# First product of an MLP on one core: both blocks of a PSUM bank filled before ScalarE empties them

## The chip, the cores and the metric

The kernel runs on one core of one Trainium2 chip. The metric is device time in microseconds: from the start of the program to its end. Beside the runs that are only timed there is one execution taken by the hardware profiler; all durations of single instructions come from it. The engines are TensorE (PE, with its weight loads shown as PEld), VectorE (DVE), ScalarE (ACT), GpSimd (POOL) and the queue SyncE (SP) that issues the transfers.

## The reference

Four layers act on an image batch of 8 x 384 x 32 x 32, each with a normalisation ahead of it and a residual. Layers 0 and 2 are Mamba blocks with a selective scan over 1024 tokens, layer 1 is a gated filter with a depthwise convolution, and layer 3 is a depthwise convolution. The change is in the MLP at the end of layer 2:

```python
# layer 2, after the scan; t: (8, 1024, 384)
t = y @ out_proj_w.T
t = jax.nn.gelu(t @ mlp_w1.T + mlp_b1, approximate=False) @ mlp_w2.T + mlp_b2
# mlp_w1: (1536, 384), mlp_w2: (384, 1536)
x = x + t
```

All data is fp32.

## The kernel before

The batch is cut into chunks of T = 512 tokens, two per image, so 16 chunks pass through layers 0 and 1 and then 16 through layers 2 and 3. Each chunk has a main line of 24 steps (`QUADS`). A step multiplies and expands (`decay`: four small matmuls into the four `dA` banks and four exponentials on ScalarE), scans (`scan`: four scans on DVE, then products on DVE and POOL) and sums over the states (`gather`: four matmuls into `y`). Everything else is a *job*: a Python generator that yields pieces, such as `front` (projections, SiLU, step sizes), `gates`, `out_proj`, `mlp` and `layer3`.

The order on each engine's queue is the order in which the Python program issues (the schedule is manual), and semaphores are set for every dependency. Between the parts of a step, `Jobs.step` lets jobs issue pieces until a planned amount of work is used (`ROOM`). It counts matmul columns (`mm`) and DVE columns (`Meter`); ScalarE's work isn't counted.

PSUM has three banks for the jobs (`psg`, `NBANK = 3`), four for `dA` and one for `y`. `pipe` runs a list of units through stages: one stage per piece. With `deep=1` a piece runs the last stage of the unit in flight and then the first stage of the next one.

The MLP of a chunk works in two halves of TH = 256 tokens. In the first product, `up(f)` is a unit for two blocks of 128 outputs. Its two stages, `run(0)` and `run(1)`, fill columns 0 to 255 and 256 to 511 of one bank `ps_up`, with three matmuls each, and each then has ScalarE add the bias and write its block to `h1` (in the trace: `h<-ps_up`). So a piece issues, in this order: the matmuls of a unit's second block, its eviction, the matmuls of the next unit's first block, its eviction. Six units make a half. Then Gelu runs over `h1` in two instructions, with a load of its table before and of the exponential's table after (`exp_again`), and the second product (`ps_dn`) uses the result.

Weights come from HBM in parts of 384 KB (`mw`, four buffers); `take` hands one to a unit and asks for the part three further on. `mm` issues every matmul from line 177 and `act` every activation from line 241, so the profile is read by tile names. An fp32 matmul leaves two records in the trace.

Of the kernel before, what the change touches and what calls it, by code (L numbers as in the profile page):

```python
# [11 lines left out]
AF = mybir.ActivationFunctionType  # L12
# [41 lines left out]
def _flat(ap):  # L54
    return ap.rearrange("p a b -> p (a b)")
# [100 lines left out]
def tile_conv_preact_d4(ctx: ExitStack, tc: tile.TileContext, a: dict, out: bass.AP):  # L156
# [15 lines left out]
    def mm(out_, lhsT, rhs, start=True, stop=True):  # L172
        columns = 1
        for n in rhs.shape[1:]:
            columns *= n
        work[0] += columns / 600
        nc.tensor.matmul(out_, lhsT, rhs, start=start, stop=stop)  # L177
# [11 lines left out]
    def pipe(units, deep=2):  # L189


        flying = []
        units = deque(units)
        while units or flying:
            went = bool(flying)
            for f in list(flying):
                if f["stages"]:
                    f["stages"].popleft()(f["ps"])
                settle(f)
                if not f["stages"]:  # L200
                    flying.remove(f)
            if units and live["ps"] < NBANK and len(flying) < deep:
                went = True
                name, stages = units.popleft()
                live["ps"] += 1
                ps = psg.tile([P, 512], F32, tag="ps", name=name)
                stages[0](ps)
                f = {"stages": deque(stages[1:]), "ps": ps, "bank": True}
                settle(f)
                if f["stages"]:  # L210
                    flying.append(f)
            if units or flying:
                yield None if went else WAIT
# [8 lines left out]
    def both(*stages):  # L222


        def run(ps):
            for stage in stages:
                stage(ps)

        return run
# [3 lines left out]
    def act(out_, in_, func, **kw):  # L233

        if func in (AF.Exp, AF.Ln):
            if act_set["now"] != "exp":
                nc.scalar.preload_act_table_set(SET_EXP)
                act_set["now"] = "exp"
        elif func not in (AF.Identity, AF.Copy, AF.Square, AF.Abs):
            act_set["now"] = func  # L240
        nc.scalar.activation(out_, in_, func, **kw)  # L241

    def exp_again():

        nc.scalar.preload_act_table_set(SET_EXP)
        act_set["now"] = "exp"
# [610 lines left out]
    TH = T // 2  # L857
# [33 lines left out]
    def mlp(s):  # L891
        x = s["x"]
        loaded, more = s["weights"]
        first = True

        def take():

            nonlocal first
            if not first:
                more()  # L900
            first = False
            return loaded.popleft()

        for half in range(2):
            cols = slice(half * TH, (half + 1) * TH)
            h1 = p2.tile([P, NF, TH], F32, tag="h1", name="h1")

            def up(f):
                def run(q):
                    def run_q(ps):  # L910
                        if q == 0:
                            now[0] = take()
                        cols_q = slice(q * TH, (q + 1) * TH)
                        for k in range(KC):
                            mm(
                                ps[:, cols_q], now[0][:, q * KC + k, :],
                                s["t"][k][:, cols], start=k == 0, stop=k == KC - 1,
                            )
                        act(
                            h1[:, f + q, :], ps[:, cols_q], AF.Identity,  # L920
                            bias=b1[:, f + q : f + q + 1],
                        )

                    return run_q

                now = [None]
                return [run(0), run(1)]

            yield from pipe([("ps_up", up(f)) for f in range(0, NF, 2)], deep=1)
            yield EARLY  # L930
            for q in range(2):
                part = _flat(h1[:, q * NFH : (q + 1) * NFH, :])
                act(part, part, AF.Gelu)
            exp_again()
            yield NEXT

            def down(m):
                def sum_up(g, third):
                    def run(ps):
                        if third == 0:  # L940
                            now[0] = take()
                        for f in range(third * KC, (third + 1) * KC):
                            mm(
                                ps[:, :TH], now[0][:, f, :], h1[:, g * NFH + f, :],
                                start=g == 0 and f == 0, stop=g == 1 and f == NFH - 1,
                            )

                    return run

                now = [None]  # L950

                def add(ps):
                    xc = x[:, m, cols]
                    vector.scalar_tensor_tensor(
                        xc, ps[:, :TH], b2[:, m : m + 1], xc, ALU.add, ALU.add
                    )

                return [sum_up(0, 0), sum_up(0, 1), sum_up(1, 0), both(sum_up(1, 1), add)]

            yield from pipe([("ps_dn", down(m)) for m in range(KC)], deep=1)  # L960
# [46 lines left out]
    for t in range(total):  # L1007
# [19 lines left out]
        if t > 0:  # L1027
            p, q = steps[t - 1]
# [4 lines left out]
        if t + AHEAD < total:  # L1033
            p, q = steps[t + AHEAD]
# [138 lines left out]
```

## Time and profile before

| | |
|---|---|
| median of 3 runs | 7943.65 us (7939.29 to 7958.2) |
| the profiled execution | 7942.61 us, span 7940.8 us |
| mean granted TensorE clock, profiled execution | 0.919 |
| PE / DVE / ACT / POOL busy | 7334.3 / 5717.7 / 4052.0 / 5639.5 us |
| first and last `ps_up` matmul | 4094.5 us, 7849.5 us |
| `ps_up` matmuls, records and busy time | 2304, 605.4 us |
| `h<-ps_up` evictions | 384 of 474 ns mean, 177.3 us |

The span is the time between the first and last instruction that the profile shows; the 1.8 us that the execution is longer lie around it. Busy time is a union of the records of one engine. PE's ends are modelled, so a busy PE isn't PE at its peak. The last figures of a group's row in the profile are the engine's idle time just before the group's instructions and what ended most of it. The granted clock is the share of full speed at which TensorE ran.

### The profile page before, as it was taken

The page shows a single profiled execution, that of the slowest core. Times are in us where ns is not written, and L with a number is a line of the kernel's source. Part 1 is how long each engine was busy: PE and PEld are TensorE (multiplying, and loading weights), DVE is VectorE, ACT ScalarE, POOL GpSimd, SP SyncE. Part 2 cuts the span into 40 slices and gives each one's busy share as a digit, 9 for nine tenths or more (in the row PEclk, how much of TensorE's full clock was granted, in tenths as well). Part 3 has the DMA queues.
Part 4 walks back from the last instruction along what each step waited for, and adds up shares of the span by engine and source line. Part 5 has one row for each costly group of instructions (what it writes and reads, how often), then busy time and mean ns, then how long its engine had stood idle before and what let it go on. Part 6 is the DMA issues. An engine that isn't in the chain of part 4 may idle for free. (4 is left out here: it accounts for less than half of the span.)

```text
span 7940.8 us, 76871 instructions
## 1 busy us (share of the span) xinstructions
PE 7334.3 (92%) x25954; PEld 3037.2 (38%) x25954; DVE 5717.7 (72%) x7254; ACT 4052.0 (51%) x6980; POOL 5639.5 (71%) x2710
## 2 busy tenths in 40 slices
PE   7989999999998999989999989999899989999898
PEld 2223333333333333333334444444444444344445
DVE  5988788878787878778737647767767676676770
ACT  4445545555555555554544545555555555555553
POOL 5888888877787878777737746767767667676770
PEclk8888888989898999989889989999999999999999
DMA  5665655555564656556526645666656666565662
GB/s 138 148 148 137 144 135 136 134 133 137 133 149 118 146 129 143 122 141 151 122 69 173 159 121 144 154 158 165 157 134 163 166 149 159 138 171 140 168 157 65
DMA packets 289704, 1122.90 MB, mean 141 GB/s; under 512 B 37402, under 2 KB 91754, under 8 KB 191004
## 3 DMA queue, kind: packets, MB, share of 16 engines
q1 hardware_dynamic: 289308, 1117.98, 57.2%
q8 instruction: 205, 3.36, 0.2%
q14 instruction: 191, 1.56, 0.1%
HBM read 1042.34 MB, written 75.50 MB: 141 GB/s over the span
## 5 line engine op out<-in xcount | busy, mean ns | idle before, releaser
L623 POOL TENSOR_TENSOR g<-g,bc 128x1024 f32<-128x1024 f32 x1536 | 3586.5, 2357 | 181.3 <-DMA g<-dud 164.4
L660 POOL TENSOR_TENSOR g<-g,bc 128x1024 f32<-128x1024 f32 x768 | 1805.8, 2351 | 1609.5 <-DVE carry L656 871.8
L241 ACT ACTIVATE dA<-dA,w_A 128x512 f32<-128x512 f32 x3072 | 1858.3, 661 | 1480.3 <-PE dA L177 1467.3
L177 PE MATMUL dA<-dt,selr 32*128 32x512 f32 x6144 | 1521.9, 676 | 67.8 <-DVE g L654 59.2
L643 DVE TENSOR_TENSOR_SCAN dA<-dA,carry,g 128x512 f32<-128x512 f32 x768 | 986.7, 1285 | 750.5 <-issue 375.4
L643 DVE TENSOR_TENSOR_SCAN dA<-dA,g 128x512 f32<-128x512 f32 x768 | 940.8, 1225 | 554.3 <-ACT dA L241 221.6
L654 DVE TENSOR_TENSOR g<-dA,bc 128x512 f32<-128x512 f32 x1536 | 1054.5, 687 | 29.8 <-DVE dA L643 0.5
L177 PE MATMUL y<-g,sely 128*32 128x512 f32 x6144 | 934.2, 640 | 47.6 <-POOL g L660 42.4
L643 DVE TENSOR_TENSOR_SCAN g<-dA,carry,g 128x512 f32<-128x512 f32 x768 | 940.4, 1266 | 0.0
L643 DVE TENSOR_TENSOR_SCAN g<-dA,g 128x512 f32<-128x512 f32 x768 | 893.7, 1206 | 0.0
L177 PEld LDWEIGHTS dA<-dt,selr 32*128 32x128 f32 x6144 | 452.1, 192 | 947.2 <-DVE g L643 473.9
L177 PE MATMUL ps_up<-t,mw 128*128 128x256 f32 x2304 | 605.4, 411 | 144.4 <-ACT h L241 100.5
L177 PE MATMUL ps_dn<-h,mw 128*128 128x256 f32 x2304 | 566.1, 397 | 67.7 <-DMA mw<-in_l_mlp_w 55.9
L177 PE MATMUL ps_z<-xf,w_in 128*128 128x512 f32 x1152 | 590.0, 653 | 27.8 <-DVE dt L85 24.0
L177 PE MATMUL ps_dw<-tp,diag 96*96 96x512 f32 x1152 | 580.7, 645 | 14.3 <-ACT diag L241 14.3
L177 PEld LDWEIGHTS ps_up<-t,mw 128*128 128x128 f32 x2304 | 444.9, 201 | 371.0 <-ACT h L241 186.7
L177 PE MATMUL ps_in<-xf,w_in 128*128 128x512 f32 x1152 | 556.2, 623 | 25.3 <-DVE u L85 22.0
L177 PE MATMUL ps_out<-u,w_out 128*128 128x512 f32 x1152 | 548.7, 623 | 9.1 <-DVE x L85 9.1
L177 PEld LDWEIGHTS ps_dn<-h,mw 128*128 128x128 f32 x2304 | 436.7, 196 | 260.3 <-issue 121.0
L177 PE MATMUL ps_dw<-xp,diag 128*128 128x512 f32 x864 | 405.4, 620 | 41.0 <-ACT diag L241 40.9
L241 ACT ACTIVATE h<-ps_up,vec 128x256 f32<-128x256 f32 x384 | 177.3, 474 | 442.7 <-PE ps_up L177 442.4
L241 ACT ACTIVATE u<-ps_in,w_vec 128x512 f32<-128x512 f32 x192 | 149.4, 778 | 478.1 <-PE ps_in L177 478.1
(98 smaller groups left out, 6514.5 us busy)
## 6 DMA issues: line engine op xcount, KB each, us to landing
g<-dud SPq DMA_DIRECT2D x768, 1024.0 KB, 7.1
mw<-in_l_mlp_w SPq DMA_DIRECT2D x384, 384.0 KB, 7.2
dud<-du SPq DMA_DIRECT2D x768, 64.0 KB, 1.7
xk<-in_x SPq DMA_DIRECT2D x48, 256.0 KB, 4.1
xf<-in_x SPq DMA_DIRECT2D x16, 768.0 KB, 8.5
x<-in_x SPq DMA_DIRECT2D x16, 768.0 KB, 8.4
x_mid<-x SPq DMA_DIRECT2D x16, 768.0 KB, 4.7
xk<-x_mid SPq DMA_DIRECT2D x48, 256.0 KB, 5.4
```

Source lines behind the costliest of these rows:

```text
L177: nc.tensor.matmul(out_, lhsT, rhs, start=start, stop=stop)
L241: nc.scalar.activation(out_, in_, func, **kw)
L623: nc.gpsimd.tensor_mul(g, g, s["bc"][:, 0, :].unsqueeze(1).to_broadcast([P, 2, T]))
L643: nc.vector.tensor_tensor_scan(dAs[j] if j < own else g[:, j, :], dAs[j], g[:, j, :], 0.0 if s["c"] == 0 else carry[:, q : q + 1], ALU.mul ...
L654: nc.vector.tensor_mul(g[:, j, :], dAs[j], s["bc"][:, 1, :])
L660: nc.gpsimd.tensor_mul(g, g, s["bc"][:, 1, :].unsqueeze(1).to_broadcast([P, 4 - own, T]))
```

## The change

In `up`, the two evictions leave the stages that fill the blocks and are issued together, behind the second block's matmuls. A piece now issues: the matmuls of a unit's second block, both its evictions, the matmuls of the next unit's first block. What is computed, the tiles and the number of instructions stay the same.

```diff
@@ def up(f): @@
                                 ps[:, cols_q], now[0][:, q * KC + k, :],
                                 s["t"][k][:, cols], start=k == 0, stop=k == KC - 1,
                             )
+
+                    return run_q
+
+                def evict(ps):
+                    for q in range(2):
                         act(
-                            h1[:, f + q, :], ps[:, cols_q], AF.Identity,
+                            h1[:, f + q, :], ps[:, q * TH : (q + 1) * TH], AF.Identity,
                             bias=b1[:, f + q : f + q + 1],
                         )
 
-                    return run_q
-
                 now = [None]
-                return [run(0), run(1)]
+                return [run(0), both(run(1), evict)]
 
             yield from pipe([("ps_up", up(f)) for f in range(0, NF, 2)], deep=1)
```

`both` runs its stages one after the other on the same bank.

## The prediction

> **What bounds the kernel now.** First the page: busy shares, then the granted TensorE clock.
>
> ```profile
> PE 7334.3 (92%) x25954; PEld 3037.2 (38%) x25954; DVE 5717.7 (72%) x7254; ACT 4052.0 (51%) x6980; POOL 5639.5 (71%) x2710
> ...
> PEclk8888888989898999989889989999999999999999
> ```
>
> TensorE is busy for 92% of the span, no other engine for more than 72%. A busy PE isn't yet a limit, so I looked at the stretch in which the changed loop runs (from 4094 us; each row: length, then busy time of PE, PEld, DVE, ACT, POOL, then clock, DMA share, GB/s), and at what PE waits for there.
>
> ```profile
> 4094.00:7870.00 3776.00, 3449.04 (x13393) 1672.21 (x13392) 2508.79 (x3201) 1916.52 (x3150) 2475.44 (x1183) 0.95 0.60 151
> ```
>
> ```profile
> PE ps_up L177 <- ACT h L241: 100.5, 77, 4.8
> PE ps_dn L177 <- DMA mw<-in_l_mlp_w: 55.9, 28, 6.3
> PE ps_dw L177 <- ACT diag L241: 40.9, 16, 4.6
> PE ps_up L177 <- DMA mw<-in_l_mlp_w: 38.6, 31, 4.1
> ```
>
> PE idles 327 us of 3776; DVE and POOL are at 66%. So PE sets this half, and the longest entry in its list of waits (total, times, longest) is the first product waiting for its own eviction: 100.5 us in 77 places. DMA is busy 60%.
>
> The costliest groups give a yardstick. Both products of the MLP issue 1152 matmuls of one shape (two records each):
>
> ```profile
> L177 PE MATMUL ps_up<-t,mw 128*128 128x256 f32 x2304 | 605.4, 411 | 144.4 <-ACT h L241 100.5
> L177 PE MATMUL ps_dn<-h,mw 128*128 128x256 f32 x2304 | 566.1, 397 | 67.7 <-DMA mw<-in_l_mlp_w 55.9
> ```
>
> With idle time, `ps_up` takes 749.8 us and `ps_dn`, which has no eviction in mid-bank, 633.8: 116 us apart.
>
> Then the timeline. PE's own timeline over the stretch gives all 77 stalls: 11 of 0.40 us, 41 of 0.56 to 0.62, 11 of 1.27, one of 2.33, and 13 of 4.08 to 4.76. The 0.56 us kind, at the end of the kernel:
>
> ```profile
> 7789.80 2.86 PE L177 MATMUL ps_up<-t,mw 128*128 128x256 f32 x12 [0.56 <-ACT h L241]
> 7792.70 0.47 ACT L241 ACTIVATE h<-ps_up,vec 128x256 f32<-128x256 f32 x1 [0.82 <-PE ps_up L177]
> 7793.23 2.86 PE L177 MATMUL ps_up<-t,mw 128*128 128x256 f32 x12 [0.57 <-ACT h L241]
> ```
>
> Second block of one unit and first of the next run as one group of 12 records; then PE stands until ScalarE has emptied that first block (0.47 us and the hand-over). The 4 us kind:
>
> ```profile
> 5623.17 1.07 PE L177 MATMUL y<-g,sely 128*32 128x512 f32 x8
> 5623.94 2.86 ACT L241 ACTIVATE u<-u 128x1536 f32<-128x1536 f32 x2
> ...
> 5626.81 1.28 ACT L245 ACT_TABLE_LOAD   x1
> 5628.11 0.84 ACT L241 ACTIVATE h<-ps_up,vec 128x256 f32<-128x256 f32 x2
> 5629.00 5.44 PE L177 MATMUL ps_up<-t,mw 128*128 128x256 f32 x12 [4.76 <-ACT h L241]
> ```
>
> Here the eviction stands in ScalarE's queue behind the SiLU of `u` and its table loads. And the 12 records after it take 5.44 us, not 2.86: the clock has fallen. The granted clock, by stretches, is 1.00 before and 0.71 after:
>
> ```profile
> 5614.00:5624.00 10.00, 10.00 (x46) 4.51 (x44) 9.76 (x13) 5.43 (x10) 7.84 (x4) 1.00 0.57 127
> 5624.00:5632.00 8.00, 3.24 (x11) 2.47 (x8) 4.92 (x5) 4.95 (x6) 5.32 (x4) 0.71 0.61 153
> ```
>
> [...] the 13 stalls over 4 us are followed by groups of 4.54 to 5.49 us, those of 1.27 us by the usual 2.86. [...] Here 6 records take 1.56 us and 12 take 2.86, so a broken group costs 0.26 us more than an unbroken one.
>
> **The change part by part.** No instruction is added or removed: 1152 matmuls and 384 evictions of 474 ns stay. The built order of the changed kernel is the same as before on PE, DVE, POOL and SP (the planner counts matmul and DVE columns only). On ScalarE, each first-block eviction moves to behind the second block's matmuls. In the semaphores, 165 of 192 second blocks wait for their own first eviction before, none after. First blocks get explicit waits instead: 65 for the eviction two units back, 17 three back, 2 one back, 26 for an eviction of `ps_in`, all of which stood earlier in ScalarE's queue.
>
> Gains, against the profiled execution (7942.6 us, span 7940.8; 1.0 below the median of 7943.65):
> - The idle time itself: 4.4 + 23.1 + 14.0 + 2.3 + 56.6 = 100.4 us.
> - Filling anew: at the 41 places of 0.56 to 0.62 us two groups become one: 41 x 0.26 = 10.7 us. At the others a `y` product stands between, nothing.
> - The clock: the 13 groups after long stalls take 4.54 to 5.49 us instead of 2.86, together 30.8 us more, and the one after 2.33 us 0.9 more: 31.8 us. I take all of it[...]. Bounds: 0 if the clock falls there for another wait, 36 if the matmuls after these groups recover too.
>
> Sum 142.9 us. What comes back:
> - In 13 SiLU places PE now runs through the 12 records and meets the `dA` products, which wait for the scans. From the timeline at 5623: PE would be there at about 5628, the last scan ends at 5629.0; other instances are closer. 13 x 0.5 = 6.5 us (0 to 13).
> - Behind them the product `ps_x` gains a wait for the delayed evictions, in 12 places: in the instance near 4343 us PE would be there at 4346.8, the evictions end at 4347.3. 12 x 0.5 = 6 us (0 to 12).
> - Weights: each unit takes 384 KB, 7.2 us from issue to landing, asked for three units ahead. Three unbroken units last 7.8 us instead of 10.3, so more of them come late; 11 of the 41 places are at the end, where DMA does nothing else. I take 10 us; 0 below, 25 above (the other 30 places, 0.83 us each, lost).
> - The last eviction before each Gelu ends 0.47 us later; uncovered only in the last two halves: 1 us. Elsewhere in the body other work covers it.
> - 5 us for waits that PE reaches sooner and that I can't name (0 to 10).
>
> Queued behind a moved eviction on ScalarE are only the exponentials of `dA`, which DVE's scans await. Before, the next unit's first eviction stood ahead of them; now one that can already run does, so they come no later: nothing, with DVE at 66% as cover.
>
> 142.9 - 28.5 = 114.4 us, close to the yardstick's 116. 7942.6 - 114.4 + 1.0 = **7829 us**.
>
> **The rivals.**
> 1. *The weight stream takes over* (chance 0.16): the body's gains turn into waits for `mw`, and the clock falls for those. For it: 94.5 us of such waits exist, some beside a stall. Against: the largest stalls aren't beside any. Giving up the clock (32), the 30 places (25) and half the long stalls (28) leaves about 58 us: 7886.
> 2. *PE doesn't set the pace, or the wait stays* (0.04): scans or POOL would fill the time, and only the end gains, 11 x 0.83 - 1 = 8 us: 7936. Against: PE's waits for DVE and POOL in this half are a few us each. That the second blocks keep their wait is excluded by the semaphores.
> 3. *Slower: banks are held longer* (0.02). There are three banks in `psg`; a unit now gives its bank back with the second of two evictions queued together, 0.47 us later. The 65 first blocks that wait two units back would each lose 0.47 + 0.26, 47 us, and the old stall would only move by three matmuls. With the end's gain of 8: about 7983. It decides from a ScalarE backlog of over 2.6 us (the 12 records between) at most units; the trace has such backlogs in 14 places, and at the 13 of SiLU the bank asked for was emptied before the SiLU.
>
> **How the numbers follow.** The main case (0.78) is 7829. Its bounds run from 7797 (all 142.9 and the further 4 of the clock) to about 7865; with rival 1 the range goes to 7886. A measurement of this kernel can tell 0.3%, 24 us, from no change; the main case and rival 1 are beyond it: faster 0.94, same 0.04, slower 0.02.
>
> **What would show it.** Right: PE's list of waits has no `ps_up` on `ACT h` beyond a few us; `ps_up` with idle time near 630 us, its mean record near 395 ns; the tail's stalls gone, one unit each 2.6 us; the clock of this half at 0.96. Wrong: `ps_up` or `ps_dn` on `mw` grow by over 25 us, `ps_x` or `dA` by over 15, or the records after the SiLU places still take over 5 us.

## The result, and the profile after

The changed kernel takes 7803.1 us in the median of 4 runs (7798.52 to 7812.56), beside 7946.2 us (7939.29 to 7958.2) for the kernel before. The ratio is 0.982, with a 95% interval of 0.9803 to 0.9837: 130 to 157 us faster. The forecast was 7829 us, in a range from 7797 to 7886.

The profiled execution of the changed kernel took 7812.56 us (span 7810.8), the slowest of the four. It is 130.1 us shorter than the profiled execution before, so the lines below account for 130 us of the 143 between the medians.

Engine busy time on its page:

```profile
PE 7294.7 (93%) x25954; PEld 3031.5 (39%) x25954; DVE 5709.7 (73%) x7254; ACT 4028.9 (52%) x6980; POOL 5636.4 (72%) x2710
```

The stretch of the changed loop, as a window (length, busy time by engine, clock, DMA share, GB/s), and what PE waits for from 4080 us to the end:

```profile
4094.00:7740.00 3646.00, 3411.10 (x13392) 1664.50 (x13391) 2506.24 (x3201) 1895.53 (x3150) 2474.49 (x1183) 0.96 0.62 156
```

```profile
PE ps_dn L177 <- DMA mw<-in_l_mlp_w: 57.5, 26, 4.4
PE ps_dw L177 <- ACT diag L241: 40.9, 16, 4.6
PE ps_lv L177 <- ACT sq L241: 34.4, 12, 3.0
PE ps_up L177 <- DMA mw<-in_l_mlp_w: 33.6, 27, 4.0
...
PE ps_up L177 <- ACT h L241: 4.5, 3, 2.7
```

The stretch is 130 us shorter for the same instructions. PE idles 235 us of it instead of 327, and is busy 38 us less. The wait that led the list, 100.5 us in 77 places, is down to 4.5 us in 3. The two products of the MLP, from the costliest groups:

```profile
L177 PE MATMUL ps_dn<-h,mw 128*128 128x256 f32 x2304 | 572.6, 400 | 70.3 <-DMA mw<-in_l_mlp_w 57.5
...
L177 PE MATMUL ps_up<-t,mw 128*128 128x256 f32 x2304 | 565.1, 394 | 50.3 <-DMA mw<-in_l_mlp_w 33.6
```

`ps_up` takes 615.4 us with its idle time, 134 less than before, and is now below `ps_dn`. The other matmul groups of this stretch move by 11 us at most, `dA` furthest.

The timelines show the two kinds of stall gone. At the end of the kernel, PE runs a whole half of the first product as one group, 72 records in 15.79 us:

```profile
7665.99 15.79 PE L177 MATMUL ps_up<-t,mw 128*128 128x256 f32 x72
```

Before, that half stretched from 7787.69 to 7808.47 us, 20.8 us. And behind the SiLU of `u`, the place shown in the prediction (rows of PE and ACT alone):

```profile
5579.31 1.07 PE L177 MATMUL y<-g,sely 128*32 128x512 f32 x8
5580.07 2.86 ACT L241 ACTIVATE u<-u 128x1536 f32<-128x1536 f32 x2
5580.30 4.15 PE L177 MATMUL ps_up<-t,mw 128*128 128x256 f32 x18
5582.94 1.28 ACT L245 ACT_TABLE_LOAD   x1
5584.24 2.29 ACT L241 ACTIVATE h<-ps_up,vec 128x256 f32<-128x256 f32 x6
5584.39 1.88 PE L177 MATMUL dA<-dt,selr 32*128 32x512 f32 x8
```

PE runs the next 18 records while ScalarE is still at the SiLU; six evictions then follow in one go. The clock over this place stays at 1.00 (before: 0.71):

```profile
5581.00:5589.00 8.00, 8.00 (x32) 4.25 (x31) 5.85 (x6) 7.95 (x14) 5.34 (x3) 1.00 0.77 182
```

What came back is in the last line of that timeline: the `dA` products take 1.88 us. Before, they took 1.14, since PE reached them only after the scans had ended:

```profile
5636.49 1.14 PE L177 MATMUL dA<-dt,selr 32*128 32x512 f32 x8
```

### The profile page after: what moved, and what is told of

Same layout as the page of the kernel before. It is cut to its first block, busy times and chain, and to the rows that moved or that the text cites. A ratio compares the mean times of both kernels' runs of the same rounds, so it can differ in the third digit from the quotient of the medians.

```text
span 7810.8 us, 76959 instructions
## 1 busy us (share of the span) xinstructions
PE 7294.7 (93%) x25954; PEld 3031.5 (39%) x25954; DVE 5709.7 (73%) x7254; ACT 4028.9 (52%) x6980; POOL 5636.4 (72%) x2710
## 3 DMA queue, kind: packets, MB, share of 16 engines
q14 instruction: 190, 1.56, 0.1%
## 5 line engine op out<-in xcount | busy, mean ns | idle before, releaser
L177 PE MATMUL ps_up<-t,mw 128*128 128x256 f32 x2304 | 565.1, 394 | 50.3 <-DMA mw<-in_l_mlp_w 33.6
L177 PE MATMUL ps_in<-xf,w_in 128*128 128x512 f32 x1152 | 554.8, 621 | 23.6 <-DVE u L85 16.6
L177 PE MATMUL ps_dw<-xp,diag 128*128 128x512 f32 x864 | 403.6, 617 | 42.2 <-ACT diag L241 40.9
L177 PEld LDWEIGHTS y<-g,sely 128*32 128x32 f32 x6144 | 133.2, 111 | 637.7 <-issue 430.0
```

## The experiments

Theory: TensorE sets the pace, and each stall costs its idle time, a broken group, and, where it is long, the half-clock records behind it (granted clock 0.50; the windows are in the last section). Rivals: the gain is ScalarE's (evictions in pairs); the slow records have another cause; the weight stream or the number of banks takes the gain back. E1 to E4, E5 to E8 and E9 to E12 each ran on one chip beside the kernel before; its medians there were 7938.29, 7939.01 and 7935.21 us. Lists of waits are from 4080 us on unless said otherwise. A line `...` marks what is left out.

**E1, the change at the SiLU places only.**

```diff
+                silu = 17 <= s["n"] <= 29 and half == 0 and f in (
+                    (4, 6) if s["n"] <= 18 else (8, 10)
+                )
+                late = silu
...
-                return [run(0), run(1)]
+                return [run(0), both(run(1), evict) if late else run(1)]
```

(Where `late` is false, each block is evicted behind its own matmuls, as before.)

> The kernel before with the change made in 26 of 192 units only: in 13 chunks, the unit whose second block stood for 4.1 to 4.8 us behind the SiLU of u, and the unit after it. If a stall costs its idle time, its refilling and the half-clock records behind it, this takes away 56.6 us of idle time, 30.8 us of slow records and 12 small stalls of 0.83 us (10 us), and gives about 11 us back at the dA products: 86 to 97 us faster than before, near 7855 us. If the records behind the stalls were slow for another reason than the stall, 55 to 67 us faster. If PE does not set the pace there, under 20 us. The trace should show those second blocks run at once and 12 records in 2.8 us behind the y products.

Measured: 7847.4 us, ratio 0.9877 (0.9854 to 0.990), 91 us between the medians. That is the theory's sum. 26 of 192 units give most of the whole gain.

**E2, the complement.** The same kernel with `late = not silu`.

> The complement: the change in the 166 other units, not in those 26. The stalls of 0.40, 0.56, 1.27 and 2.33 us that go are worth 43.8 us of idle time, 0.9 of clock and 29 refills of 0.26 us (7.5), less the small stalls beside the SiLU places (12 x 0.56): about 45 us faster than before, near 7900 us. If the gains of the two kernels add up, they give the 143 us of the whole change. If small stalls are covered by other waits (weights, scans), it is under 20 us and the two don't add up to 143.

Measured: 7904.51 us, ratio 0.9958 (0.9941 to 0.9975), 34 us between the medians. The 45 us that I expected lie within its interval (20 to 47). E1 and E2 together make 1.65%, against 1.77 to 1.8% for the whole change; within their intervals the parts add up. So the small stalls weren't covered by other waits.

**E3, early evictions, a bank for each block.**

```diff
                         if q == 0:
                             now[0] = take()
+                        else:
+                            ps = psg.tile([P, 512], F32, tag="ps", name="ps_up")
```

> The kernel before, evictions where they were (each right behind its own block), but the second block goes to a bank of its own. If the cost was that a second block shares the bank of the eviction that it waits for, this is as good as the change: 130 to 145 us faster than before, near 7803 us, with hardly a wait of ps_up for h in PE's list. If the gain came from ScalarE's side (evictions in pairs, exponentials sooner), it gains under 30 us. If banks become short (each block now takes one of three), PE waits for evictions two blocks back: 60 to 110 us faster.

Measured: 7851.9 us, ratio 0.9879 (0.9859 to 0.9899), 86 us between the medians: the case of short banks. From PE's list of waits:

```profile
...
PE ps_up L177 <- DVE dt L85: 54.3, 36, 3.0
...
PE ps_up L177 <- ACT h L241: 27.3, 13, 2.5
```

Most of the gain comes although every eviction stands where it stood before, so pairing the evictions isn't what gains; not sharing the bank is (waits for evictions: 27.3 us in 13 places, instead of 100.5 in 77). But the blocks now compete for three banks, and wait for the step-size job (`dt`), which holds one, and in the 13 SiLU places for an eviction further back. A bank for each block is worth 86 us here; keeping both blocks in one bank and emptying it afterwards gives 143.

**E4, the stall filled with idle work.** All waits of the kernel before are kept.

```diff
+                        elif silu and live["ps"] < NBANK:
+                            idle = psg.tile([P, 512], F32, tag="ps", name="ps_idle")
+                            for _ in range(9):
+                                nc.tensor.matmul(
+                                    idle[:, :TH], now[0][:, 0, :], s["t"][0][:, cols],
+                                    start=True, stop=True,
+                                )
```

(`silu` as in E1, but only the first of the two units.)

> The kernel before, all waits kept; in the 13 chunks, nine matmuls of 256 columns (about 3.9 us) into another bank, whose result is not used, stand ahead of the second block that is held up behind the SiLU of u. They fill the stall. If the half clock behind the stalls is caused by the idle time, the 12 records behind them take 2.9 instead of 4.5 to 5.5 us: 13 x 2.4 us, 25 to 31 us faster than before although PE does more work, near 7918 us. If those records are slow for another reason, or their slowness costs nothing, 0 to 5 us slower.

Measured: 7899.6 us, ratio 0.9941 (0.9925 to 0.9958): 33 to 60 us faster, 39 between the medians, with 54 us more work on PE. Its timeline at one of the places (rows of PE and ACT alone), and its group of the first product:

```profile
5602.78 4.15 PE L916 MATMUL ps_idle<-t,mw 128*128 128x256 f32 x18
5605.43 1.28 ACT L245 ACT_TABLE_LOAD   x1
5606.72 0.84 ACT L241 ACTIVATE h<-ps_up,vec 128x256 f32<-128x256 f32 x2
5607.61 2.86 PE L177 MATMUL ps_up<-t,mw 128*128 128x256 f32 x12 [0.69 <-ACT h L241]
...
L177 PE MATMUL ps_up<-t,mw 128*128 128x256 f32 x2304 | 571.1, 393 | 84.7 <-ACT h L241 49.7 <-DMA mw<-in_l_mlp_w 26.9 <-DVE dt L85 5.8
```

The second block here still starts when its eviction ends, but its 12 records take 2.86 us, not 5.44, and so do those at the other 12 places. The first product's records take 34.3 us less than before in all. So it was the idle time that had slowed them; the mean granted clock of the profiled execution is 0.924, beside 0.919 before.

**E5, the changed kernel again**, beside the next three.

> The changed kernel again, beside the next three on one chip. 0.980 to 0.984 of before.

Measured: 7796.08 us, ratio 0.9823 (0.9806 to 0.9841).

**E6, diagonals further ahead**, on the changed kernel.

```diff
+        ahead = 6 if rows == P else 3
...
-                d = pool.tile([P, rows], F32, tag="diag", name="diag", bufs=4)
+                d = pool.tile([P, rows], F32, tag="diag", name="diag", bufs=ahead + 1)
...
-            ready.append(diagonal(q + 3))
+            ready.append(diagonal(q + ahead))
```

> The changed kernel, and in layer 3 ScalarE prepares the diagonal weights of the depthwise convolution six taps ahead instead of three. In the changed kernel ps_dw waits 40.9 us for them in 16 places, 4.57 us at a time where a table switch stands before them on ScalarE, with slow records after. Three more taps give 1.3 us more cover: if PE's waits for ScalarE cost idle time and clock as in the first product, 7 x (1.3 + 1.7) and 8 x 1.2, about 15 to 30 us faster than the changed kernel. If those places are covered by other work, no difference.

Measured: 7793.57 us, ratio 0.9816 (0.980 to 0.9833): no difference from E5. The wait did shrink, and in the profiles another grew. E6's list of waits:

```profile
PE ps_dn L177 <- DMA mw<-in_l_mlp_w: 67.1, 32, 5.0
PE ps_up L177 <- DMA mw<-in_l_mlp_w: 40.9, 36, 4.2
...
PE ps_dw L177 <- ACT diag L241: 13.5, 10, 2.7
```

`ps_dw` on `diag` fell from 40.9 to 13.5 us; the weights' two entries rose from 85.5 us (58.9 and 26.6 in E5) to 108. In one profile of each, that is most of the expected gain; two profiles of the changed kernel differ by 5.6 us in these two entries.

**E7, squares of the layer norm in a piece of their own**, on E6.

```diff
...
+        sqs = [square(k) for k in range(2)]
+        yield NEXT
         ps = yield from ps_tile("ps_lv")
         for k in range(KC):
-            sq = wk.tile([P, T], F32, tag="spm", name="sq", bufs=2)
-            act(sq, xn[:, k, :], AF.Square)
-            mm(ps, ln_mean, sq, start=k == 0, stop=k == KC - 1)
+            mm(ps, ln_mean, sqs[k], start=k == 0, stop=k == KC - 1)
+            if k == 0:
+                sqs.append(square(2))
...
```

(`square(k)` makes the tile as before. The left-out lines have a job wait until the two buffers of the squares are free.)

> The kernel of the diagonals ahead, and in the layer norm of layer 2 two of the three squares that ScalarE makes for ps_lv are issued one piece before the matmuls that use them (the third needs a free buffer and stays). In the changed kernel ps_lv waits 34.4 us for them in 12 places of 3.0 us, with records of 4.5 to 5.5 us in place of 2.8 after. By the same price for a stall, 12 x (2.1 + 1.5 to 2) = 40 to 50 us faster than the diagonals ahead alone. If the longer front of a chunk (one piece more) makes others late, no gain, or up to 30 us slower.

Measured: 7984.46 us, ratio 1.0058 (1.0038 to 1.0078): slower than the kernel before, far outside what I expected. The wait of `ps_lv` fell to 9.3 us, but the added piece moves the planner's later pieces (in the trace, PE's tiles follow each other in another order at about 200 places), and others rise: `ps_in` on DVE's `u` from 8.9 to 76.5 us, the weights from 108 to 150.8:

```profile
PE ps_dn L177 <- DMA mw<-in_l_mlp_w: 89.8, 27, 7.4
PE ps_in L177 <- DVE u L85: 76.5, 33, 4.3
PE ps_up L177 <- DMA mw<-in_l_mlp_w: 61.0, 17, 5.5
```

**E8, banks kept longer**, on the changed kernel.

```diff
-                return [run(0), both(run(1), evict)]
+                return [run(0), run(1), evict]
-            yield from pipe([...], deep=1)
+            yield from pipe([...])
```

> The changed kernel with the two evictions as a stage of their own, a piece later, two units in flight: every bank is kept a piece longer. If three banks are enough, as the changed kernel suggests, it is within 15 us of the changed kernel. If the banks are near their limit, PE waits for evictions and for other users of the banks, and it is 30 to 80 us slower than the changed kernel, as with a bank for each block.

Measured: 8134.69 us, ratio 1.0246 (1.0228 to 1.0265), 339 us slower than E5; I had the direction as an alternative, but not its size. The longest of PE's waits over its whole execution, where E5 has 16.6 and 5.4 us:

```profile
PE ps_in L177 <- DVE u L85: 162.8, 57, 4.3
PE ps_up L177 <- ACT h L241: 118.4, 43, 3.5
```

With two units in flight the projections `ps_in` have one bank left and wait out each other's taps on DVE. The edit also adds a piece to each half, as E7 added one to a chunk; but in E8's trace PE goes through its tiles in the order of the changed kernel, except for some 90 us near 4650 us, so a changed order isn't the cause. The third rival of the prediction, banks held longer, is thus a real mechanism. One piece more brings it; the 0.47 us of the change don't.

**E9, the squares at the end of the piece before**, on the changed kernel: as E7, but the two squares follow DVE's subtractions ahead of the `yield NEXT` that was there, so TensorE's order is unchanged (the trace has it so). Diagonals are three ahead, as in the changed kernel.

> The changed kernel; two of the three squares for ps_lv are issued at the end of the piece before, behind DVE's subtractions, so the chunk has no piece more and TensorE's order is that of the changed kernel. If a stall of 3.0 us costs its idle time and slow records behind it, as in the first product, 12 x (2.1 + 1.5 to 2) = 40 to 50 us faster than the changed kernel, and the loss of the squares with a piece of their own came from the piece. If the squares standing earlier in ScalarE's queue are what costs, slower than the changed kernel.

Measured: 7774.37 us, ratio 0.9787 (0.977 to 0.9804) beside 0.9823 for E5: about 29 us faster than the changed kernel, less than the 40 to 50 expected. `ps_lv` waits 11.9 us instead of 34.4. Ten waits of `ps_up` on `t` came up in their place, 12.0 us. So squares that stand earlier on ScalarE aren't what E7 lost by. What is left of its edit is the extra piece and the order that followed from it; the diagonals ahead made no difference in E6.

**E10, five buffers for the weights**, on the changed kernel; layer 3 adds in place to make room.

```diff
-                w = p2.tile([P, NFH, P], F32, tag="mw", name="mw", bufs=4)
+                w = p2.tile([P, NFH, P], F32, tag="mw", name="mw", bufs=5)
...
-        for _ in range(4):
+        for _ in range(5):
             more()
...
-                    acc = p2.tile([P, T], F32, tag="acc", name="acc")
-                    vector.tensor_add(acc, ps, x[hf][:, k, :])
-                    nc.sync.dma_start(out[b, k * P : (k + 1) * P, rows], acc)
+                    xc = x[hf][:, k, :]
+                    vector.tensor_add(xc, ps, xc)
+                    nc.sync.dma_start(out[b, k * P : (k + 1) * P, rows], xc)
```

> The changed kernel with five buffers for the MLP's weights instead of four, so each part is asked for four ahead; for the space, layer 3 adds its result in place and sends it from there. TensorE's order is that of the changed kernel. If its waits for weights (85 to 91 us in all) are bound by the look-ahead, half or more of them goes: 40 to 80 us faster than the changed kernel with their half-clock records. If the transfers' rate or the order on SP's queue sets them, under 15 us.

Measured: 7716.77 us, ratio 0.9719 (0.9697 to 0.9741), some 83 us faster than the changed kernel by the two ratios. The in-place addition alone was not run; E12 goes without it. The waits for weights:

```profile
PE ps_up L177 <- DMA mw<-in_l_mlp_w: 13.9, 10, 3.6
PE ps_dn L177 <- DMA mw<-in_l_mlp_w: 13.5, 10, 2.6
```

**E11, E9 and E10 together.**

> The squares in the same piece and five weight buffers together, on the changed kernel: if the gains add up, 80 to 130 us faster than the changed kernel, near 7690 us; if removing one stall feeds the other wait, less than the larger of the two plus 10 us.

Measured: 7683.84 us, ratio 0.968 (0.9661 to 0.9699): the fastest kernel here, 251 us (3.2%) below the kernel before in the median. E9 took 0.36% off the changed kernel's ratio, E10 1.04%, both together 1.43%: they add up.

**E12, three buffers for the weights**, on the changed kernel: the first four lines of E10's edit with 3 for 5.

> The changed kernel with three weight buffers instead of four: each part is asked for two ahead, 5.2 us of unbroken matmuls, against 7.0 us to landing. If the look-ahead sets the waits for weights, they rise by 100 us or more and it is 100 to 250 us slower than the changed kernel. If it doesn't, under 40 us slower.

Measured: 8013.23 us, ratio 1.0091 (1.0074 to 1.0108), 2.7% slower than the changed kernel. PE waits 210.4 us for weights:

```profile
PE ps_dn L177 <- DMA mw<-in_l_mlp_w: 129.0, 36, 11.2
PE ps_up L177 <- DMA mw<-in_l_mlp_w: 81.4, 36, 6.4
```

PE waits 27 us with five buffers, 91 (85.5 in E5) with four and 210 with three: the look-ahead sets these waits.

## Why the prediction was right, and where it was off

**TensorE sets this half.** Right. PE's time in the stretch fell by the same 130 us as the execution, while DVE and POOL kept their work. E1, E2 and E3 took waits away in other places or in another way, and gained each time.

**Idle time, 100.4 us.** Right: the entry fell by 96.0 us, and no other entry of `ps_up` grew by more than 4.4.

**Filling and clock, 10.7 + 31.8 us.** Right in kind: `ps_up`'s busy time fell by 40.3 us with the same records, and the group behind the SiLU ran at full clock (1.00). That all of the clock's share would go was an estimate of mine. E4 isolates the clock: the records of `ps_up` lose 34.3 us, between my 31.8 and my upper bound of 36. The kernel gains 33 to 60; whether anything beyond the records is part of that isn't shown. (At the end there are 12 of the 0.56 us stalls, not 11, which is 0.8 us.)

**The waits as they are.** Right that no second block waits on its eviction any more and that the first blocks' new waits find old evictions: 4.5 us in 3 places.

**What comes back, 28.5 us.** This term was mis-sized, and it is most of why the forecast is 26 us too slow. Its parts:
- Weights, 10 us taken (0 to 25): nothing. The two entries were 94.5 us before and 91.1 after (85.5 in E5; 79.8 in E1 and 94.0 in E2). The premise was sound: E12 and E10 show that the look-ahead sets these waits. But no profile of the change, or of a part of it, has them longer than before. Why not is open.
- `ps_x` behind the delayed evictions, 6 us: 0.2 us, once. I had read it from one place, near 4343 us, and taken it for 12; that place alone has the wait. In the instance shown above, PE is held at the `dA` products until the evictions are nearly done.
- `dA` waiting for scans, 6.5 us (0 to 13): 5.0 us, all of it in the records. At the 13 places the `dA` products take 1.88 us five times, 1.38 five times and 1.14 to 1.24 three times, instead of 1.14. I had looked for it in the idle column only. (Over the stretch the group's records grew by 10.6 us, 510.0 to 520.6; the other 5.6 us lie elsewhere.)
- Gelu in the last two halves, 1 us: 10.1 to 11.2 us, as forecast.
- Unnamed, 5 us: rises and falls of other groups, which cancel.

In the two profiles the first product gained 96.0 + 40.3 = 136.3 us (142.9 forecast), and the returns named took 6.3. That makes 130.0, and the two executions differ by 130.1, where 114.4 was forecast. The other 10 us of the 26 are no fault of the mechanism: the profiled execution of the changed kernel lies 9.5 us above its median, and the forecast had added 1.0. Bounding each return from both sides was right, since the result lies in the range. Taking the weights and `ps_x` from the middle of their bounds, 16 us, was the error.

**The rivals.** The weight stream did not take over here, though E6's profile has it doing just that to another gain. The rival of no pace-setting PE falls with E1 and E2. The slower case, banks held longer, didn't come; E8 and E3 show what it costs when it does.

## What to carry to other kernels

Look for the wait with which the pacing engine stands on a helper, sort its places by length, and see what stands ahead of the helper's instruction in its queue: here 13 of 77 places, behind one SiLU, gave most of the gain. Issue the work that doesn't depend on the helper first, in the same bank, and let the helper empty the bank once, but don't hold a scarce buffer for a piece longer. When such a stall is gone, ask which wait is next before shortening another: for this kernel it was the weights' look-ahead, and one buffer more, with the in-place addition that made room for it, was worth 1%.

## What the runs showed of the hardware that I had not expected

Matmuls whose result nobody uses made the kernel faster. In E4, 54 us of them in place of idle time brought the 12 records behind each long stall from 4.5 to 5.5 us down to 2.86, and the kernel gained 33 to 60 us. That is about 3 us for each of 13 stalls (39 us between the medians, divided by 13), beside the 4 to 5 us of the stall itself. The granted clock, in the kernel before, at the stall from 5624.24 to 5629.00 us that the prediction shows (columns as in the windows above):

```profile
5624.50:5627.00 2.50, 0.00 (x0) 0.00 (x0) 2.47 (x4) 2.48 (x3) 1.92 (x1) 1.00 0.66 184
5627.50:5634.00 6.50, 5.00 (x12) 3.87 (x12) 1.46 (x2) 1.91 (x4) 4.90 (x3) 0.50 0.50 116
5634.50:5640.00 5.50, 5.00 (x20) 2.20 (x21) 1.57 (x2) 3.27 (x6) 1.55 (x1) 1.00 0.01 2
```

In windows of 0.1 us, the clock falls from 1.00 to 0.50 at each of the 13 long stalls of the kernel before and at the one of 2.33 us, 2.5 to 5.1 us after PE's last record ahead of the stall. It stays there for 3.5 us in four places, where it fell only when PE was at work again, and for about 7 us in ten. At the 11 stalls of 1.27 us it stays at 1.00.

Shorter waits can have slow records behind them too. In E3, 11 groups of 12 records stood behind a wait of 1.89 or 2.47 us for an eviction: eight took 4.38 to 4.54 us, three 2.86.

```profile
5372.45 4.50 PE L177 MATMUL ps_up<-t,mw 128*128 128x256 f32 x12 [1.89 <-ACT h L241]
```

Among the 77 stalls of the kernel before is one such case, the one of 2.33 us: 6 records behind it take 2.50 us instead of 1.56, while none of the 11 of 1.27 us has slow records behind it. What decides between 1.3 and 4 us isn't shown.
